# Q transposed on VectorE in 32 x 32 squares and carried through DRAM: one edit to a two-stage attention kernel

## The chip, the cores and the metric

The kernel runs on one core of one Trainium2 chip. The metric is the device time of one execution in microseconds (us); the number for a kernel is the median of several runs. Profiles come from one more execution, recorded by the hardware profiler; its span runs from the first to the last instruction.

## The reference, cut to what matters

The input is 4 sequences of 512 tokens with 128 features. First comes a pre-norm causal attention layer with 16 heads of 64 (stage 1). Then come six layers (stage 2), each a windowed attention followed by a feed-forward block:

```
for i in range(6):
    x = attn_layer(shift_tokens(x), Wqkv[i], q_scale[i], k_scale[i], Wo[i]) + x
    x = ffn_layer(shift_tokens(x), ln_g[i], ...) + x

attn_layer:  q, k, v = split(x @ Wqkv)          # 128 -> 3 x (16 heads x 64)
             q = l2norm(q) * q_scale ; k = l2norm(k) * k_scale   # per head
             q, k = rotary with a per-position scale
             window w of 32 queries sees the keys of windows w-1 and w,
             (keys at most 32 back, none ahead), softmax, times v
             out @ Wo
```

All of it is f32. The edit is in stage 2's attention: how Q is brought into the layout that the scores need, how V is laid out by windows, and on which engine the inverse of the l2 norm is begun.

## The kernel before

Stage 1 takes the first 550 us and is not touched. Stage 2 works in units: a unit is 128 tokens of one sequence in one layer, so there are 6 x 4 x 4 = 96. The order of all instructions is written out by hand: `slot(n, ...)` (L900) issues one slot, and in it four units at different ages: the scores, softmax and values of unit n (`u`), the output projection of n - 1 (`prev`), the last steps of Q and K of n + 1 (`nxt`), and the projections and rotary of n + 2 (`new`). Pieces of the feed-forward block are put into slots by the dictionaries `norm`, `move` and `geglu` (L996 on). Each engine carries out its instructions strictly in the order in which they are issued, so an instruction that waits holds back all that is behind it on its engine. There are four units to a sequence, so slots come in fours.

The way of one unit:

- `project` (L535): six f32 products of 128 x 512 on TensorE for Q, K and V (two instructions each, L538), tokens on the partitions of the result.
- `square` (L550) on ScalarE and `sum_squares` (L555) on VectorE: the sums for the norms.
- `rotate` (L558; L560 and L566) on VectorE and `add_rotated` (L577) on GpSimd: the rotary.
- `inverse_norms` (L579): VectorE clamps the 32 sums of each token (L581) and computes the bit-trick seed of the inverse square root (L83, L84 in `rsqrt`), then GpSimd does three Newton steps of four small operations (L86 to L89). `over_norm` (L584, L585) multiplies on GpSimd, first Q, then K.
- `transpose_q` (L661) and `transpose_k` (L666): eight 128 x 128 transposes on TensorE each (L656), copied out of PSUM by ScalarE (L659). `qT` has the head's features on the partitions and one buffer. The first 32 key columns of `kT` are carried over from the unit before (`carry_k`, L672).
- `scores` (L677): the band mask is put into PSUM by eight bf16 products (L683, the first TensorE instructions of a slot), then 128 small products (L694) add the scores: for each pair of heads `c`, window `j` and head of the pair `h`, 32 queries by 64 keys. VectorE takes the maximum (L704) and subtracts it (L706), ScalarE the exponents (L712).
- `v_windows` (L627): ScalarE copies V out of PSUM into `vt` (L638), tokens on the partitions, with a column of ones beside each head; sixteen DMAs on SyncE's queue (SP) then copy blocks of 32 tokens from SBUF to SBUF into `vw`, so that each window has the keys of the window before and its own on neighbouring partitions. The last window's keys go into the next unit's `vw` as well. `vw` has three buffers, and the first unit of a sequence has its own, `vw_first`, whose missing window is zero.
- `times_v` (L719): 128 small products (L726), VectorE divides by the column of ones (L735, L736), `transpose_o` (L743) and `project_out_2` (L748, L751) follow, `residual` (L753; L759) on VectorE.

In the order of a slot: scores of u, projection 0 of new, exponents of u, the norms of the unit that the slot before left over, feed-forward norm steps, output projection of prev, rotary 0 of new, transposed probabilities of u between the halves of projection 1 of new, `times_v` of u, rotary 1 of new, `transpose_q` of nxt, projection 2 of new, `transpose_k` of nxt, `v_windows` of new, `carry_k`, feed-forward pieces, `transpose_o` of u.

Tiles of one tag share buffers in turn: `t1` has four, taken by the two squares and the two rotary products of a unit.

Of the kernel before, what the change touches and what calls it, by code (L numbers as in the profile page):

```python
# [23 lines left out]
W = 32  # L24
# [8 lines left out]
def body(ctx: ExitStack, tc: tile.TileContext, a, out: bass.AP):  # L33
# [15 lines left out]
    small = ctx.enter_context(tc.tile_pool(name="small", bufs=4))  # L49
    def tmpt(n=S):  # L50
        return tmp.tile([P, n], F32, tag="tmp", name="tmp_t")
# [128 lines left out]
    with tc.manual_schedule():  # L180
# [218 lines left out]
        def residual1(b, y):  # L399
            nc.vector.tensor_tensor(x1T[b], y, x0T[b], ALU.add)  # L400
# [88 lines left out]
    s2a = ps2a = s2b = s2 = ps_one = kT_first = vw_first = vts = None  # L489
# [89 lines left out]
    def inverse_norms(u):  # L579

        nc.vector.tensor_scalar(u.ss, u.ss, 1e-24, None, ALU.max)  # L581
        rsqrt(u.ss, 2 * HEADS, nc.gpsimd)
# [16 lines left out]
    def second_step():  # L599

        nonlocal s2b, ps_one, kT_first, vw_first, vts
        steps[1].close()
        s2b = ctx.enter_context(tc.tile_pool(name="s2b", bufs=1))
        ps_one = ctx.enter_context(tc.tile_pool(name="ps2b", bufs=1, space=PSUM))


        vts = [s2b.tile([P, 2, NC, HD + 1], F32, tag=f"vt{j}", name=f"vt{j}") for j in range(2)]
        for t_ in vts:
            nc.gpsimd.memset(t_[:, :, :, HD : HD + 1], 1.0)
        vw_first = s2b.tile([P, NW, NC, HD + 1], F32, tag="vw_first", name="vw_first")  # L610
        for c in range(2):
            nc.gpsimd.memset(vw_first[c * HD : c * HD + W, 0], 0.0)
        kT_first = s2b.tile([P, NC, W + P], F32, tag="kT_first", name="kT_first")
        nc.gpsimd.memset(kT_first[:, :, 0:W], 0.0)
# [12 lines left out]
    def new_vw(u):  # L627
        if u.T == 0:
            return vw_first
        return s2b.tile([P, NW, NC, HD + 1], F32, tag="vw", name="vw", bufs=3)  # L630

    def v_windows(u, nxt):


        vt = vts[u.n % 2]
        src = u.p[2].rearrange("p (c a d) -> p a c d", a=2, d=HD)
        for c in range(2):
            nc.scalar.copy(vt[:, c, :, 0:HD], src[:, c])  # L638
        if u.T == 0:
            u.vw = new_vw(u)  # L640
        if nxt is not None:
            nxt.vw = new_vw(nxt)
        for j in range(NW):
            rows = slice(j * W, (j + 1) * W)
            for c in range(2):
                nc.sync.dma_start(out=u.vw[c * HD + W : (c + 1) * HD, j], in_=vt[rows, c])
                if j + 1 < NW:
                    nc.sync.dma_start(out=u.vw[c * HD : c * HD + W, j + 1], in_=vt[rows, c])
                elif nxt is not None:
                    nc.sync.dma_start(out=nxt.vw[c * HD : c * HD + W, 0], in_=vt[rows, c])  # L650
# [10 lines left out]
    def transpose_q(u):  # L661
        u.qT = s2b.tile([P, NC, P], F32, tag="qT", name="qT", bufs=1)
        for g in range(2):
            transposed(u.r[0], g, u.qT, 0)
# [12 lines left out]
    def scores(u):  # L677
# [13 lines left out]
        for c in range(NC):  # L691
            for j in range(NW):
                for h in range(2):
                    mm(  # L694
                        sc[j * W : (j + 1) * W, h, c * 2 * W : (c + 1) * 2 * W],
                        lhsT=u.qT[h * HD : (h + 1) * HD, c, j * W : (j + 1) * W],
# [174 lines left out]
    def first_slot():  # L871
# [26 lines left out]
        v_windows(new, units[1])  # L898

    def slot(n, norm, move, geglu):  # L900
# [47 lines left out]
        if n == -1:  # L948
            residual1(B - 1, y)
        if u:  # L950
            times_v(u, 0)
            times_v(u, 1)
# [7 lines left out]
        if nxt:  # L960
            transpose_q(nxt)
        if new:
            do_project(new, 2, 0, 2 if geglu else 1)
        if new and geglu:
            v_windows(new, follower(new))
        if nxt:
            transpose_k(nxt)
        if new and not geglu:
            do_project(new, 2, 1)
            v_windows(new, follower(new))  # L970
# [116 lines left out]
def _constants(n):  # L1087
# [41 lines left out]
    return {"tabs": tabs, "band": band, "pen": pen, "ident16": ident16}  # L1129
# [49 lines left out]
```

## Time and profile before

| what | us |
|---|---|
| median of 3 runs (2192.52 to 2196.64) | 2193.21 |
| span of the profiled execution | 2189.6 |
| TensorE (PE) busy in it | 2137.6 |
| VectorE (DVE) | 1721.8 |
| GpSimd (POOL) | 1509.3 |
| ScalarE (ACT) | 1381.4 |

The runs' time is 3.6 us above the span; no run's time was taken of the profiled execution itself, so this is how the two stand to each other. Mean granted TensorE clock: 0.994 of full speed. DMA moved 125.77 MB, 57 GB/s over the span.

How to read it: a group of instructions is named by its line, engine, operation and tiles (`out<-in`), with how many there were, their busy time and the mean of one; behind the bar stands the idle time of the engine just before them and what ended it. PE are the products, PEld the loads of their stationary operand, which run beside products. The chain is followed back from the last instruction: at each step to what released it, or to the instruction before it on its engine. In an answer in order of time, a row has start, length, engine, line and operation; in brackets stands the idle time before it with its releaser. In a table by stretches, a row has the stretch and its length, then busy us and number of instructions for PE, PEld, DVE, ACT and POOL, the granted TensorE clock, the busy share of the DMA engines, and GB/s.

### The profile page before, as it was taken

What the parts mean: (1) busy time and instruction counts of PE and PEld (TensorE: products, weight loads), DVE (VectorE), ACT (ScalarE), POOL (GpSimd) and SP (SyncE); (2) the same over time, 40 slices, a digit from 0 to 9 for tenths busy, and PEclk for the clock granted to TensorE, in tenths of its full rate; (3) what the DMA queues carried; (4) which work ended last, traced back from release to release, by engine and by line L of the source; (5) the groups of instructions that cost most, each with busy time, mean ns of one, the idle gap of its engine ahead of it and who ended that gap; (6) DMA issues with size and microseconds to landing.
All of it is one profiled execution on the core that took longest, in us unless ns stands there. A gap on an engine that the chain in (4) does not pass through costs nothing.

```text
span 2189.6 us, 82509 instructions
## 1 busy us (share of the span) xinstructions
PE 2137.6 (98%) x35150; PEld 1432.0 (65%) x35150; DVE 1721.8 (79%) x2501; ACT 1381.4 (63%) x2677; POOL 1509.3 (69%) x2281
## 2 busy tenths in 40 slices
PE   7999999999999999999999999999999999999998
PEld 5665555555666666766666666766666666666665
DVE  4766766667778888888888888888888888888884
ACT  4665656665455667766667666676666676666763
POOL 2554545555787787787787777877787777778772
PEclk8999999999999999999999999999999999999999
DMA  3000000000322232232332223323232233323220
GB/s 121 1 1 1 1 1 1 1 1 1 77 64 66 66 93 73 70 74 61 92 78 64 72 68 93 75 62 78 67 100 65 65 76 83 86 65 74 62 71 26
DMA packets 91064, 125.77 MB, mean 57 GB/s; under 512 B 25422, under 2 KB 39500, under 8 KB 90700
## 3 DMA queue, kind: packets, MB, share of 16 engines
q1 hardware_dynamic: 89996, 118.79, 21.8%
q8 instruction: 280, 4.59, 0.9%
q10 hardware_dynamic: 704, 1.70, 0.2%
q14 instruction: 84, 0.69, 0.1%
HBM read 20.31 MB, written 1.05 MB: 10 GB/s over the span
## 4 chain that ended last, share of the span: by engine, by line
PE 89%; DVE 7%; POOL 2%; issue 1%; ACT 1%; DMA 0%; SPq 0%; POOLq 0%; DVEq 0%; ACTq 0%
PE ps_proj L538 21%; PE ps_one L656 15%; PE ps_one L751 7%; PE ps_att L726 6%; PE ps_att L694 6%; PE ps_sc L298 6%; PE ps_o L383 5%; PE ps_pt L363 5%; PE ps_proj L815 3%; PE ps_proj L795 3%; PE ps_proj L796 3%; PE ps_att L683 1%; PE ps_pj L277 1%; PE ps_pj L267 1%; PE ps_pj L261 1%
## 5 line engine op out<-in xcount | busy, mean ns | idle before, releaser
L577 POOL TENSOR_TENSOR rot<-rot,t 128x1024 f32<-128x1024 f32 x192 | 454.2, 2366 | 179.6 <-DVE t L566 161.9
L538 PE MATMUL ps_proj<-wqkv,xs 128*128 128x512 f32 x1152 | 569.3, 602 | 1.8 <-issue 1.3
L352 POOL TENSOR_TENSOR pr<-pr,den 128x1024 f32<-128x1024 f32 x128 | 240.9, 1893 | 247.5 <-DVE den L349 237.7
L585 POOL TENSOR_TENSOR rot<-rot,ss 128x1024 f32<-128x1024 f32 x192 | 361.8, 1905 | 7.4
L550 ACT ACTIVATE sq<-ps_proj 128x1024 f32<-128x1024 f32 x192 | 196.5, 1024 | 177.1 <-PE ps_proj L538 152.7
L538 PEld LDWEIGHTS ps_proj<-wqkv,xs 128*128 128x128 f32 x1152 | 188.2, 190 | 104.8 <-issue 95.0
L560 DVE TENSOR_TENSOR rot<-ps_proj,lt 128x1024 f32<-128x1024 f32 x192 | 233.7, 1217 | 6.8 <-ACT sq L550 6.5
L566 DVE TENSOR_TENSOR t<-ps_proj,lt 128x1024 f32<-128x1024 f32 x192 | 233.1, 1214 | 0.0
L555 DVE TENSOR_REDUCE ss<-sq 128x16 f32<-128x1024 f32 x192 | 232.2, 1210 | 0.0
L338 ACT ACTIVATE pr<-ps_sc,nm 128x128 f32<-128x128 f32 (+3 forms) x448 | 220.3, 509 | 11.8 <-DVE nm L325 8.6
L656 PEld LDWEIGHTS ps_one<-ident,rot 128*128 128x128 f32 x1536 | 173.0, 141 | 71.1 <-issue 46.8
L656 PE MATMUL ps_one<-ident,rot 128*128 128x128 f32 x1536 | 207.5, 278 | 9.2 <-POOL rot L585 4.9
L325 DVE TENSOR_REDUCE nm<-ps_sc 128x2 f32<-128x1024 f32 x128 | 155.9, 1218 | 62.9 <-PE ps_sc L313 62.9
L751 PEld LDWEIGHTS ps_one<-aT,wo 128*128 128x128 f32 x1536 | 182.9, 192 | 23.7 <-issue 21.1
L659 ACT COPY pT<-ps_one 128x512 f32<-128x512 f32 x192 | 110.1, 586 | 136.8 <-PE ps_one L656 136.8
L751 PE MATMUL ps_one<-aT,wo 128*128 128x128 f32 x1536 | 189.1, 276 | 0.4 <-DVE rs L113 0.3
L735 DVE RECIPROCAL rden<-ps_att 128x8 f32<-128x8 f32 x192 | 39.0, 203 | 182.1 <-PE ps_att L726 181.9
L659 ACT COPY qT<-ps_one 128x512 f32<-128x512 f32 x192 | 103.5, 589 | 108.9 <-PE ps_one L656 108.8
L638 ACT COPY vt<-ps_proj 128x512 f32<-128x512 f32 x192 | 103.2, 590 | 98.3 <-PE ps_proj L538 91.9
L86 POOL TENSOR_TENSOR yt<-y 128x32 f32<-128x32 f32 (+2 forms) x384 | 87.7, 228 | 112.1 <-DVE y L84 66.2
L363 PEld LDWEIGHTS ps_pt<-ident,pr 128*128 128x128 f32 x1024 | 117.3, 141 | 58.5 <-issue 47.7
L704 DVE TENSOR_REDUCE mx<-ps_att 128x16 f32<-128x1024 f32 x96 | 117.0, 1219 | 35.8 <-PE ps_att L694 35.5
(174 smaller groups left out, 4194.5 us busy)
## 6 DMA issues: line engine op xcount, KB each, us to landing
vw<-vt SPq DMA_DIRECT2D x1152, 65.0 KB
vw_first<-vt SPq DMA_DIRECT2D x336, 65.0 KB
wqkv<-in_wqkv_dram SPq DMA_DIRECT2D x18, 512.0 KB
wo<-in_wo_dram SPq DMA_DIRECT2D x6, 512.0 KB
w<-in_w_dram SPq DMA_DIRECT2D x6, 341.0 KB
xr<-in_x_dram SPq DMA_DIRECT2D x3, 256.0 KB
scales<-in_scales_dram SPq DMA_DIRECT2D x6, 128.0 KB
w<-in_w_dram SPq DMA_DIRECT2D x12, 64.0 KB
```

The costliest lines, as they stand in the source:

```text
L338: nc.scalar.activation(self.pr[:, h, cols], self.sc[:, h, cols], AF.Exp, bias=self.nm[:, part_, h : h + 1], accum_out=self.den[:, part_, h ...
L352: nc.gpsimd.tensor_tensor(self.pr, self.pr, self.den[:, 0].unsqueeze(2).to_broadcast([P, 2, S]), ALU.mult)
L363: nc.tensor.transpose(pt[:, k * P : (k + 1) * P], self.pr[:, h, k * P : (k + 1) * P], ident)
L538: mm(p[:, c, :], lhsT=u.xs[:, u.T * P : (u.T + 1) * P], rhs=wpart[j][:, c * 512 : (c + 1) * 512], start=True, stop=True,)
L555: nc.vector.tensor_reduce(u.ss[:, j * HEADS : (j + 1) * HEADS], heads(u.sq[j]), AX.X, ALU.add)
L560: nc.vector.tensor_tensor(heads(t0), heads(pf), lt[:, u.T, 2 * j].unsqueeze(1).to_broadcast([P, HEADS, HD]), ALU.mult)
L566: nc.vector.tensor_tensor(t1.rearrange("p (h t d) -> p h t d", t=2, d=half), pf.rearrange("p (h t d) -> p h t d", t=2, d=half)[:, :, ::-1, :],
L577: nc.gpsimd.tensor_tensor(u.r[j], u.r[j], u.t1, ALU.add)
L585: nc.gpsimd.tensor_tensor(heads(u.r[j]), heads(u.r[j]), u.ss[:, j * HEADS : (j + 1) * HEADS].unsqueeze(2).to_broadcast([P, HEADS, HD]), AL ...
L656: nc.tensor.transpose(tp[:, c * P : (c + 1) * P], src[:, (4 * g + c) * P : (4 * g + c + 1) * P], ident)
L659: nc.scalar.copy(dst[:, 4 * g : 4 * g + 4, col0 : col0 + P], tp.rearrange("p (c t) -> p c t", c=4))
L751: mm(y[:, 0:P], lhsT=wo_w[0][:, c, :], rhs=u.aT[:, c, :], start=(c == 0), stop=(c == NC - 1))
```

## The change

Three things change in stage 2.

**Q.** VectorE transposes the normalised Q in 32 x 32 squares (one instruction of 128 x 1024), into a tile `blocks` of the tag `t1`. Since a square stays on its 32 partitions, the squares still stand in the wrong places: one DMA writes all 512 KB to a DRAM tile `qd` (two buffers), and four DMAs of 128 KB read it back, each onto 32 partitions of `qT`. `qT` is now ordered by window, then pair of heads. The eight TensorE transposes and two ScalarE copies are gone. The call of `transpose_q` moves up in the slot, from behind rotary 1 of new to ahead of `times_v` of u.

**V.** `vt` is written to a DRAM tile by one DMA (rows are tokens, with 32 rows of zeros ahead of the first), and four DMAs read it into `vw`: even and odd windows, for each head of the pairs. Two DRAM tiles take turns by sequence. Every unit's `vw` now comes from the same two buffers, and nothing is put into the next unit's.

**Inverse norms.** The clamp and the seed are done by GpSimd, in one operation each, ahead of the Newton steps.

```diff
     def inverse_norms(u):
-        nc.vector.tensor_scalar(u.ss, u.ss, 1e-24, None, ALU.max)
-        rsqrt(u.ss, 2 * HEADS, nc.gpsimd)
+        v, n, eng = u.ss, 2 * HEADS, nc.gpsimd
+        eng.tensor_scalar(v, v, 1e-24, None, ALU.max)
+        y = small.tile([P, n], F32, tag=f"y{n}", name="y")
+        t = small.tile([P, n], F32, tag=f"yt{n}", name="yt")
+        eng.tensor_scalar(y.bitcast(I32), v.bitcast(I32), -0.5, 1597463007.0, ALU.mult, ALU.add)
+        for k in range(3):
+            eng.tensor_tensor(t, y, y, ALU.mult)
...
     def second_step():
...
-        vw_first = s2b.tile([P, NW, NC, HD + 1], F32, tag="vw_first", name="vw_first")
-        for c in range(2):
-            nc.gpsimd.memset(vw_first[c * HD : c * HD + W, 0], 0.0)
+        vds = [dram.tile([W + S, 2, NC * (HD + 1)], F32, tag=f"vd{j}", name=f"vd{j}") for j in range(2)]
+        for d_ in vds:
+            nc.sync.dma_start(out=d_[0:W], in_=a["zeros"])
...
-    def v_windows(u, nxt):
+    def v_windows(u):
-        vt = vts[u.n % 2]
+        vt, vd = vts[u.n % 2], vds[u.n // NT % 2]
...
-        for j in range(NW):
-            rows = slice(j * W, (j + 1) * W)
+        r0 = u.T * P
+        nc.sync.dma_start(out=vd[r0 + W : r0 + W + P], in_=vt.rearrange("p a c d -> p a (c d)"))
+        u.vw = s2b.tile([P, NW, NC, HD + 1], F32, tag="vw", name="vw", bufs=2)
+        for odd in range(2):
+            rows = vd[r0 + odd * W : r0 + odd * W + P].rearrange("(j k) a x -> a k j x", k=2 * W)
             for c in range(2):
-                nc.sync.dma_start(out=u.vw[c * HD + W : (c + 1) * HD, j], in_=vt[rows, c])
-                if j + 1 < NW:
-                    nc.sync.dma_start(out=u.vw[c * HD : c * HD + W, j + 1], in_=vt[rows, c])
-                elif nxt is not None:
-                    nc.sync.dma_start(out=nxt.vw[c * HD : c * HD + W, 0], in_=vt[rows, c])
+                nc.sync.dma_start(
+                    out=u.vw[c * HD : (c + 1) * HD, odd::2].rearrange("p j c d -> p j (c d)"), in_=rows[c]
+                )
...
     def transpose_q(u):
-        u.qT = s2b.tile([P, NC, P], F32, tag="qT", name="qT", bufs=1)
-        for g in range(2):
-            transposed(u.r[0], g, u.qT, 0)
+        blocks = s2a.tile([P, 4, NC, W], F32, tag="t1", name="blocks", bufs=4)
+        nc.vector.transpose(
+            out=blocks.rearrange("p b c d -> p (b c d)"),
+            in_=u.r[0].rearrange("p (c b d) -> p b c d", b=4, d=W),
+        )
+        qd = dram.tile([NW, W, 4, NC * W], F32, tag="qd", name="qd", bufs=2)
+        nc.sync.dma_start(out=qd.rearrange("a i b x -> (a i) (b x)"), in_=blocks.rearrange("p b c d -> p (b c d)"))
+        u.qT = s2b.tile([P, NW, NC, W], F32, tag="qT", name="qT", bufs=1)
+        for b_ in range(4):
+            nc.sync.dma_start(
+                out=u.qT[b_ * W : (b_ + 1) * W].rearrange("p a c d -> p a (c d)"),
+                in_=qd[:, :, b_].rearrange("a i x -> i a x"),
+            )
...
     def scores(u):
...
-                        lhsT=u.qT[h * HD : (h + 1) * HD, c, j * W : (j + 1) * W],
+                        lhsT=u.qT[h * HD : (h + 1) * HD, j, c],
...
     def slot(n, norm, move, geglu):
...
+        if nxt:
+            transpose_q(nxt)
         if u:
             times_v(u, 0)
             times_v(u, 1)
...
-        if nxt:
-            transpose_q(nxt)
         if new:
             do_project(new, 2, 0, 2 if geglu else 1)
```

More of the change, by code (lines that the diff above doesn't have):

```diff
@@ L49, in body @@
     small = ctx.enter_context(tc.tile_pool(name="small", bufs=4))
+    dram = ctx.enter_context(tc.tile_pool(name="dram", bufs=1, space=bass.MemoryType.DRAM))
     def tmpt(n=S):
@@ L488, in body @@
     ps = ctx.enter_context(tc.tile_pool(name="ps2", bufs=1, space=PSUM))
-    s2a = ps2a = s2b = s2 = ps_one = kT_first = vw_first = vts = None
+    s2a = ps2a = s2b = s2 = ps_one = kT_first = vts = vds = None
     def load_part(i, j):
@@ L579, in inverse_norms @@
     def inverse_norms(u):
-        nc.vector.tensor_scalar(u.ss, u.ss, 1e-24, None, ALU.max)
-        rsqrt(u.ss, 2 * HEADS, nc.gpsimd)
+        v, n, eng = u.ss, 2 * HEADS, nc.gpsimd
[5 more added lines that the diff above has]
+            eng.tensor_tensor(t, y, y, ALU.mult)
+            eng.tensor_tensor(t, t, v, ALU.mult)
+            eng.tensor_scalar(t, t, -0.5, 1.5, ALU.mult, ALU.add)
+            eng.tensor_tensor(y if k < 2 else v, y, t, ALU.mult)
     def over_norm(u, j):
@@ L599, in second_step @@
     def second_step():
-        nonlocal s2b, ps_one, kT_first, vw_first, vts
+        nonlocal s2b, ps_one, kT_first, vts, vds
         steps[1].close()
@@ L625, in new_kT @@
         return s2.tile([P, NC, W + P], F32, tag="kT", name="kT", bufs=2)
[L627 to L630, printed above, removed]
-    def v_windows(u, nxt):
-        vt = vts[u.n % 2]
+    def v_windows(u):
+        vt, vd = vts[u.n % 2], vds[u.n // NT % 2]
         src = u.p[2].rearrange("p (c a d) -> p a c d", a=2, d=HD)
@@ L638, in v_windows @@
             nc.scalar.copy(vt[:, c, :, 0:HD], src[:, c])
[L639 to L642, printed above, removed]
-        for j in range(NW):
-            rows = slice(j * W, (j + 1) * W)
-            for c in range(2):
-                nc.sync.dma_start(out=u.vw[c * HD + W : (c + 1) * HD, j], in_=vt[rows, c])
-                if j + 1 < NW:
-                    nc.sync.dma_start(out=u.vw[c * HD : c * HD + W, j + 1], in_=vt[rows, c])
-                elif nxt is not None:
-                    nc.sync.dma_start(out=nxt.vw[c * HD : c * HD + W, 0], in_=vt[rows, c])
+        r0 = u.T * P
[3 more added lines that the diff above has]
+            rows = vd[r0 + odd * W : r0 + odd * W + P].rearrange("(j k) a x -> a k j x", k=2 * W)
+            for c in range(2):
+                nc.sync.dma_start(
+                    out=u.vw[c * HD : (c + 1) * HD, odd::2].rearrange("p j c d -> p j (c d)"), in_=rows[c]
+                )
     def transposed(src, g, dst, col0):
@@ L897, in first_slot @@
         do_project(new, 2)
-        v_windows(new, units[1])
+        v_windows(new)
     def slot(n, norm, move, geglu):
@@ L964, in slot @@
         if new and geglu:
-            v_windows(new, follower(new))
+            v_windows(new)
         if nxt:
@@ L969, in slot @@
             do_project(new, 2, 1)
-            v_windows(new, follower(new))
+            v_windows(new)
         if n == -1:
@@ L1128, in _constants @@
     ident16 = np.eye(P).astype(ml_dtypes.bfloat16)
-    return {"tabs": tabs, "band": band, "pen": pen, "ident16": ident16}
+    zeros = np.zeros((W, 2, NC * (HD + 1)), f)
+    return {"tabs": tabs, "band": band, "pen": pen, "ident16": ident16, "zeros": zeros}
 def kernel(**inputs):
```

## The prediction

> **What bounds the kernel now.** I read the page first, then the chain of work that ended last, then the groups, then the order in time of one slot, and last the places where TensorE stood still.
>
> ```profile
> span 2189.6 us, 82509 instructions
> PE 2137.6 (98%) x35150; PEld 1432.0 (65%) x35150; DVE 1721.8 (79%) x2501; ACT 1381.4 (63%) x2677; POOL 1509.3 (69%) x2281
> PE 89%; DVE 7%; POOL 2%; issue 1%; ACT 1%; DMA 0%; SPq 0%; POOLq 0%; DVEq 0%; ACTq 0%
> ```
>
> PE is busy for 98% of the span and is 89% of the chain; DMA is nothing in it. So an instruction that leaves PE shortens the kernel, as long as no wait takes its place. The layers are 96 slots, one per unit of 128 tokens; a slot begins with the band matmuls of L683. From the first (559.71) to the last (2149.78) it is 1590 us, 16.74 us for each of 95 slots. They come in fours of 15.87, 16.85, 17.49 and 16.26 us (medians).
>
> The order in time of the slot that starts at 1226.24, by engine (start, length, line):
>
> ```profile
> 1226.24 0.41 PE L683 MATMUL ps_att<-band,ident 64*32 64x512 bf16 x8
> 1226.47 1.69 PE L694 MATMUL ps_att<-kT_first,qT 64*32 64x64 f32 x128
> 1234.39 1.59 PE L726 MATMUL ps_att<-vw_first,pT 64*32 64x65 f32 x128
> 1235.91 1.09 PE L656 MATMUL ps_one<-ident,rot 128*128 128x128 f32 x8
> 1236.84 1.88 PE L538 MATMUL ps_proj<-wqkv,xs 128*128 128x512 f32 x4
> 1242.11 0.41 PE L683 MATMUL ps_att<-band,ident 64*32 64x512 bf16 x8
> ...
> 1230.04 1.23 DVE L706 TENSOR_TENSOR pr<-ps_att,mx 128x1024 f32<-128x1024 f32 x1
> 1231.23 1.23 DVE L560 TENSOR_TENSOR rot<-ps_proj,lt 128x1024 f32<-128x1024 f32 x1
> 1232.37 0.28 DVE L759 TENSOR_TENSOR xT<-ps_one,xT 128x128 f32<-128x128 f32 x1
> 1232.57 1.22 DVE L566 TENSOR_TENSOR t<-ps_proj,lt 128x1024 f32<-128x1024 f32 x1
> 1235.41 0.21 DVE L735 RECIPROCAL rden<-ps_att 128x8 f32<-128x8 f32 x1 [1.62 <-PE ps_att L726]
> ...
> 1232.16 3.76 POOL L585 TENSOR_TENSOR rot<-rot,ss 128x1024 f32<-128x1024 f32 x2
> ```
>
> Two things are to be seen. The eight Q transposes hold PE from 1235.91 to 1236.84. And Q is wanted early: it is normalised by the first half of L585 (to 1234.0), and the next scores read it at 1242.3.
>
> **Part 1: off PE and ACT.** The Q transposes go: 0.93 us a slot, 95 x 0.93 = 88 us, all of it on the chain. (By the chain's share, 15% on L656's 3072 transposes, it is 0.107 x 8 = 0.86 us.) PE alone would need 16.74 - 0.93 = 15.81 us. ACT loses two qT copies (0.59 us each); it has gaps in every slot, so I count nothing.
>
> **Part 2: clamp and seed to GpSimd.** DVE loses L581 (1.36 us mean), L83 (0.26) and L84 (0.20), 1.8 us a slot. GpSimd gains two small operations, at 0.22 us (L88) and a gap of 0.1 each about 0.6 us, and no longer waits for DVE's seed. GpSimd is busy some 13 of 16.7 us. PE waits for neither; I count nothing by itself. It lets DVE begin L704 as soon as the scores end; that enters below.
>
> **Part 3: V through DRAM.** 15.5 DMAs of 65 KB a unit become one write of 520 KB and four reads of 130 KB. V is made two slots before L726 reads it: with about 9 us for write and reads (below) against over 25 us, it is hidden. SP issues ten DMAs a slot instead of 15.5. Queued order on SP matters: Q's write and reads stand ahead of V's, and V's of the slot before are done (write 4 us after its copy, four issues of 0.6 us) some 4 us into the next slot, before Q's write is wanted. Cost nothing; without that cover V would cost as much as Q does.
>
> **Part 4: Q's new way, which is the forecast.** DVE's transpose waits for L585, SP's write waits for the transpose, the four reads wait for the write, and the scores, at the head of PE's queue, wait for the reads; all PE work of the slot is queued behind them. Counted from a slot's first PE instruction:
>
> - DVE ends L566 at 7.5, 8.3, 7.9 and 7.55 us in the four kinds of slot. In the first two DVE came late to L704 (2.54 and 2.78 against 2.0, behind L581); without that the mean is 7.5. Q's L585 ends at 7.8, 8.1, 7.35 and 6.6, and since GpSimd does not wait for PE here, each us by which PE is late takes one off: it ends first once PE waits. So 7.5.
> - The transpose, 128x1024 f32, is not in the trace. Nearest: L555, one input of that size, 1.21 us. Below: L125, SBUF to SBUF, 0.57 for half the size, so 1.1. Above: GpSimd's 2.37, or a wait as of L581, which takes 0.17 us with GpSimd idle and up to 2.26 beside it. I take 1.2: 8.7 us. It stands ahead of L735, where DVE idles anyway (1.62 us above).
> - The write of 512 KB to DRAM. Nearest: the last output, 256 KB in two DMAs, first issued at 2186.43; the bytes move from 2187.25 to 2188.4 and the span ends at 2189.6, 3.2 us after the issue. Another 256 KB at its 290 GB/s is 0.9: 4.1. Below: the 0.85 us to the first byte, 1.8 us of bytes and the 0.5 us between last byte and reader that the scales load shows: 3.15.
> - Four reads of 128 KB. An issue takes 0.6 (L646), so the fourth starts 1.8 us after the first. From issue to reader: 3.3 us for the 128 KB of scales (two rows below, behind a V transfer), 2.8 for the first load of x (0.75 to 3.55). I take 1.8 + 3.0 = 4.8; bounds 1.35 + 2.8 = 4.15 (issues of 0.45 as at the start) and 5.3.
>
> ```profile
> 1839.45 0.54 SPq L170 DMA_DIRECT2D scales<-in_scales_dram  x1
> 1842.73 2.37 POOL L172 TENSOR_TENSOR lt<-tabs,scales 128x1024 f32<-128x1024 f32 x1 [1.36 <-DMA scales<-in_scales_dram]
> 2186.43 0.90 SPq L836 DMA_DIRECT2D out_dram<-rot  x2
> ```
>
> Sum: 8.7 + 0.1 + 4.1 + 4.8 = 17.7 us from one slot's scores to the next. That is more than PE's 15.8 and more than today's 16.74. The loop closes through DVE (scores, L704, L706, L560, L566, transpose), so a late start is not made up. PE would stand still for 17.7 - 15.8 = 1.9 us at each slot's head.
>
> **What such a stop does to PE's clock.** The trace has 26 stops over 0.7 us. After the 1.90 us before 2145.36, the 2.84 before 8.60 and the 2.91 before 673.99 the granted clock is 0.5 for 3 to 13 us; after those up to 1.61 us it stays 1.00.
>
> ```profile
> 671.10:674.00 2.90, 0.01 (x4) 0.01 (x4) 2.90 (x4) 1.20 (x3) 1.99 (x11) 0.97 0.32 75
> 674.00:677.00 3.00, 3.00 (x137) 2.51 (x137) 1.59 (x2) 0.00 (x0) 2.37 (x1) 0.50 0.38 89
> 677.50:680.00 2.50, 2.50 (x16) 1.74 (x15) 2.40 (x7) 1.15 (x2) 0.37 (x2) 1.00 0.45 107
> ```
>
> (The seventh number is PE's clock.) The slot at 673.99 shows the price: L566 ends 8.54 us in, against 7.55 in its kind, and the slot takes 17.59 against 16.26. So a slowed slot adds 1.0 us to the loop. Stops of 1.9 us lie at the edge; I take every second slot slowed: 18.2 us. The excess is 18.2 - 16.74 = 1.46, times 95 = 139 us. The profiled execution: 2189.6 + 139 = 2328.6; the median lies 3.6 above that span, so 2332 us.
>
> Two pages of the Trainium skill differ from these rows. "DMA: Bandwidth & Descriptors", Anatomy of one DMA, gives 2.0 us plus bytes at 436 GB/s for a DMA (of GpSimd's path): by that, an estimate, write 3.2 and last read 2.3 us; with the issues the loop is 16.1 us and the kernel some 60 us faster. "TensorE: Matmul & The Clock Gate", Part 1, lets the clock fall after an idle window of about 3.4 us: by that no stop here would slow PE, and the loop stays at 17.7; the trace has it at 0.5 after 1.9 us.
>
> **Rivals.**
> - *The transfers are quick enough (faster).* The point is the way from transpose to scores: 8.0 us gives today's slot (8.7 + 8.0), 7.1 hides it all. At the lower bounds of the rows, 0.1 + 3.15 + 4.15 = 7.4, the slot is 16.1: 95 x -0.64 = -61, 2132 us; all hidden, 2105. For it: the DMA engines are busy for 30% of the layers. Against: the two roundtrips in a row that the output and the scales show.
> - *A stop without the slow clock.* 17.7: 95 x 0.96 = +91, 2284 us. For it: stops up to 1.61 us left the clock alone, and the wait splits unevenly among slots.
> - *A longer way.* Write 4.3, reads 5.3, transpose held behind the second L585, every slot slowed: 8.7 + 1.0 + 9.7 = 19.4, and with a held transpose up to 20.6. 19.4 gives +253, 2446 us.
> - *GpSimd becomes the bound*: 13.6 us of work in a slot of 15.8 or more; I give it no share of its own.
> - *It does not do what it says*: the built order shows the eight matmuls gone, one transpose on DVE and five DMAs for Q in each slot, so no.
>
> **How the numbers follow.** Stop with the clock slowed in part (2290 to 2390): 0.46. Stop without (2200 to 2290): 0.20. Longer (above 2390): 0.16. Faster: 0.15. Equal within 0.2% (what a measurement of this kernel can tell from no change; it needs 8.0 within 0.05): 0.03. Range 2135 to 2445: from the rows' lower bounds to the longer way at 19.4. Slower by over 0.2% 0.82, same 0.03, faster 0.15.
>
> **What would show it.** Right: L694 (L705 after) waits for the qT transfer at nearly every slot's head, DMA appears in the chain, PE's share falls to about 88%, slots of about 18 us, the granted clock 0.5 in part of the slots. Transpose: about 1.2 us, ahead of the reciprocals. Write: some 4 us from issue to the first read's issue; reads 4.8 us from there to L694. Wrong: no idle time before the scores and slots below 16.7 us; or a clock of 1.00 throughout; or a wait on V or on GpSimd ahead of the one on Q.

## The result, and the profile after

The changed kernel takes 2279.73 us (median of 4 runs, 2274.09 to 2282.22) against 2192.86 us for the kernel before on the same chip: a ratio of 1.038, 95% interval 1.036 to 1.040. The forecast was 2332 us. The profiled execution's span grows from 2189.6 to 2277.5 us, by 87.9 us. Line numbers from here on are those of the changed kernel, some 10 above those of before (scores L694 and L705, maximum L715, values L737, reciprocals L746, `over_norm` L594, Q's transpose L664, its write L669 and reads L672).

The page of the changed kernel: span, busy time, DMA, the chain's shares by engine, the transpose's group, and the transfers with their time from issue to landing.

```profile
span 2277.5 us, 79327 instructions
...
PE 2092.4 (92%) x34382; PEld 1364.7 (60%) x34382; DVE 1683.3 (74%) x2309; ACT 1275.1 (56%) x2485; POOL 1555.8 (68%) x2471
...
DMA packets 157928, 280.79 MB, mean 123 GB/s; under 512 B 17006, under 2 KB 80236, under 8 KB 157548
...
PE 60%; DMA 11%; POOL 11%; DVE 10%; issue 4%; SPq 3%; ACT 1%; POOLq 0%; DVEq 0%; ACTq 0%
...
L664 DVE STREAM_TRANSPOSE blocks<-rot 128x1024 f32<-128x1024 f32 x96 | 119.0, 1240 | 29.3 <-POOL rot L594 29.2
...
qd<-blocks SPq DMA_DIRECT2D x96, 512.0 KB, 2.8
qT<-qd SPq DMA_DIRECT2D x384, 128.0 KB, 2.9
```

PE lost its 768 transposes, 88 us by the prediction's count, yet its busy time fell by only 45.2 us: the rest ran slower, at a mean granted clock of 0.979 instead of 0.994. Its idle time rose from 52 to 185 us, by 133. So 133 - 45 = 88. The chain, 89% PE before, now runs through DMA, GpSimd and VectorE for a third of its length.

Where PE stands idle, from the view of waits (us in total, times, longest):

```profile
PE ps_att L705 <- DMA qT<-qd: 77.1, 90, 6.3
...
PE ps_proj L539 <- DVE rden L746: 47.9, 76, 1.8
```

The first is the wait that was forecast: the scores wait for Q. The second was not: projection 2 of new waits for VectorE's reciprocals, which free the PSUM bank that it writes. Before, the eight Q transposes stood between `times_v` and projection 2 and covered that time. Both are seen in one slot, in order of time:

```profile
1216.48 1.51 PE L737 MATMUL ps_att<-vw,pT 64*32 64x65 f32 x128
...
1217.22 1.25 DVE L664 STREAM_TRANSPOSE blocks<-rot 128x1024 f32<-128x1024 f32 x1 [1.40 <-POOL rot L594]
...
1218.39 0.17 DVE L746 RECIPROCAL rden<-ps_att 128x8 f32<-128x8 f32 x1
...
1218.49 0.34 SPq L669 DMA_DIRECT2D qd<-blocks  x1
...
1219.43 1.95 PE L539 MATMUL ps_proj<-wqkv,xs 128*128 128x512 f32 x4 [1.44 <-DVE rden L746]
...
1221.39 1.76 SPq L672 DMA_DIRECT2D qT<-qd  x4
...
1224.78 0.41 PE L694 MATMUL ps_att<-band,ident 64*32 64x512 bf16 x8
...
1225.83 1.46 PE L705 MATMUL ps_att<-kT,qT 64*32 64x64 f32 x126 [0.55 <-DMA qT<-qd]
```

VectorE's transpose waits 1.40 us for GpSimd's normalization, and the reciprocals are queued behind it. From its end (1218.47) the write is issued at once, the first read 2.9 us later, the four reads some 0.44 us apart, and the scores go on at 1225.83: 7.4 us for the whole way.

By stretch of the layers, in the same two executions: the first eight slots took 131.9 us before and 159.8 after (+27.9), the other 87 took 1458.2 and 1509.8 (+51.6), the end behind the last scores 39.8 and 47.9 (+8.1). The mean slot is 17.57 us (16.74 before). Sixteen slots are longer than 18.6 us (one before); below they are called long. The others grew little: from the ninth slot on the medians of the four kinds are 16.50, 17.38, 17.78 and 16.10 us, in the mean 16.94 (before 16.62); this is called the ordinary slot.

### The profile page after: what moved, and what is told of

Same layout as the page of the kernel before. It is cut to its first block, busy times and chain, and to the rows that moved or that the text cites. A ratio compares the mean times of both kernels' runs of the same rounds, so it can differ in the third digit from the quotient of the medians.

```text
span 2277.5 us, 79327 instructions
## 1 busy us (share of the span) xinstructions
PE 2092.4 (92%) x34382; PEld 1364.7 (60%) x34382; DVE 1683.3 (74%) x2309; ACT 1275.1 (56%) x2485; POOL 1555.8 (68%) x2471
## 4 chain that ended last, share of the span: by engine, by line
PE 60%; DMA 11%; POOL 11%; DVE 10%; issue 4%; SPq 3%; ACT 1%; POOLq 0%; DVEq 0%; ACTq 0%
PE ps_proj L539 15%; DMA qT<-qd 7%; PE ps_sc L299 5%; PE ps_o L384 5%; PE ps_one L657 5%; PE ps_one L762 5%; PE ps_att L705 5%; PE ps_pt L364 5%; DMA qd<-blocks 4%; POOL rot L578 3%; SPq L672 3%; POOL rot L594 3%; PE ps_att L737 2%; PE ps_proj L826 2%; DVE on L747 2%
## 5 line engine op out<-in xcount | busy, mean ns | idle before, releaser
L539 PE MATMUL ps_proj<-wqkv,xs 128*128 128x512 f32 x1152 | 593.4, 624 | 52.8 <-DVE rden L746 47.9
L578 POOL TENSOR_TENSOR rot<-rot,t 128x1024 f32<-128x1024 f32 x192 | 453.3, 2361 | 240.9 <-DVE t L567 156.9
L594 POOL TENSOR_TENSOR rot<-rot,ss 128x1024 f32<-128x1024 f32 x192 | 361.7, 1905 | 7.4
L539 PEld LDWEIGHTS ps_proj<-wqkv,xs 128*128 128x128 f32 x1152 | 193.6, 195 | 174.7 <-issue 122.6
L561 DVE TENSOR_TENSOR rot<-ps_proj,lt 128x1024 f32<-128x1024 f32 x192 | 233.8, 1218 | 23.4 <-ACT sq L551 21.2
L567 DVE TENSOR_TENSOR t<-ps_proj,lt 128x1024 f32<-128x1024 f32 x192 | 233.4, 1215 | 18.8 <-POOL rot L578 18.8
L715 DVE TENSOR_REDUCE mx<-ps_att 128x16 f32<-128x1024 f32 x96 | 117.6, 1225 | 172.5 <-PE ps_att L705 172.3
L737 PEld LDWEIGHTS ps_att<-vw,pT 64*32 64x32 f32 x12288 | 131.4, 105 | 83.8 <-ACT pT L660 71.3
L705 PE MATMUL ps_att<-kT,qT 64*32 64x64 f32 x9216 | 126.0, 233 | 60.1 <-DMA qT<-qd 55.5
L737 PE MATMUL ps_att<-vw,pT 64*32 64x65 f32 x12288 | 150.4, 225 | 8.6 <-issue 8.0
L705 PEld LDWEIGHTS ps_att<-kT,qT 64*32 64x32 f32 x9216 | 111.2, 108 | 78.3 <-DMA qT<-qd 52.3
L664 DVE STREAM_TRANSPOSE blocks<-rot 128x1024 f32<-128x1024 f32 x96 | 119.0, 1240 | 29.3 <-POOL rot L594 29.2
```

Source lines behind the costliest of these rows:

```text
L539: mm(p[:, c, :], lhsT=u.xs[:, u.T * P : (u.T + 1) * P], rhs=wpart[j][:, c * 512 : (c + 1) * 512], start=True, stop=True,)
L561: nc.vector.tensor_tensor(heads(t0), heads(pf), lt[:, u.T, 2 * j].unsqueeze(1).to_broadcast([P, HEADS, HD]), ALU.mult)
L567: nc.vector.tensor_tensor(t1.rearrange("p (h t d) -> p h t d", t=2, d=half), pf.rearrange("p (h t d) -> p h t d", t=2, d=half)[:, :, ::-1, :],
L578: nc.gpsimd.tensor_tensor(u.r[j], u.r[j], u.t1, ALU.add)
L594: nc.gpsimd.tensor_tensor(heads(u.r[j]), heads(u.r[j]), u.ss[:, j * HEADS : (j + 1) * HEADS].unsqueeze(2).to_broadcast([P, HEADS, HD]), AL ...
L705: mm(sc[j * W : (j + 1) * W, h, c * 2 * W : (c + 1) * 2 * W], lhsT=u.qT[h * HD : (h + 1) * HD, j, c], rhs=u.kT[h * HD : (h + 1) * HD, c, j ...
```

## The experiments

The theory on record: Q's way to the scores is the bound (letter C in later expectations). Its rivals: the doubled traffic slows everything (B); V or the norms take a share; and, after the first four runs, that the reciprocals queued behind VectorE's transpose hold TensorE (A), and that VectorE's part of the slot is next (D). "Slot" is the mean of 95 in the profiled execution, "long" the number of slots over 18.6 us, "clock" the mean granted TensorE clock of that execution. Ratios are to the kernel before, run on the same chip.

| run | median us | ratio, 95% interval | slot | long | clock |
|---|---|---|---|---|---|
| change | 2279.73 | 1.038 (1.036 to 1.040) | 17.57 | 16 | 0.979 |
| 1 norms alone | 2181.24 | 0.994 (0.993 to 0.996) | 16.62 | 0 | 0.996 |
| 2 V alone | 2178.25 | 0.993 (0.991 to 0.994) | 16.57 | 1 | 0.995 |
| 3 Q alone | 2338.54 | 1.066 (1.064 to 1.069) | 18.16 | 32 | 0.972 |
| 4 stale Q | 2277.64 | 1.038 (1.036 to 1.040) | 17.64 | 23 | 0.975 |
| 5 stale Q, old place | 2243.19 | 1.023 (1.021 to 1.024) | 17.24 | 12 | 0.978 |
| 6 K first | 2296.98 | 1.049 (1.046 to 1.052) | 17.71 | 23 | 0.968 |
| 7 early norms | 2230.02 | 1.017 (1.015 to 1.019) | 17.11 | 7 | 0.990 |
| 8 early norms, K first | 2265.23 | 1.033 (1.030 to 1.035) | 17.41 | 17 | 0.979 |
| 9 early norms, place of the change | 2288.57 | 1.040 (1.037 to 1.043) | 17.71 | 24 | 0.973 |
| 10 norms and V | 2174.24 | 0.989 (0.987 to 0.990) | 16.53 | 1 | 0.996 |
| 11 fill in the first layer | 2281.95 | 1.039 (1.037 to 1.041) | 17.56 | 14 | 0.986 |
| 12 reads on two queues | 2274.12 | 1.035 (1.032 to 1.037) | 17.59 | 18 | 0.982 |

**Runs 1 to 3: each part alone, put into the kernel before.** Run 1 takes `inverse_norms` of the change, run 2 `second_step` and `v_windows`, run 3 `transpose_q`, its new place and the new index of `qT`:

```diff
# run 1
-        nc.vector.tensor_scalar(u.ss, u.ss, 1e-24, None, ALU.max)
-        rsqrt(u.ss, 2 * HEADS, nc.gpsimd)
+        eng.tensor_scalar(v, v, 1e-24, None, ALU.max)   # eng = nc.gpsimd
...
# run 2
-            v_windows(new, follower(new))
+            v_windows(new)
...
# run 3
+        if nxt:
+            transpose_q(nxt)
         if u:
             times_v(u, 0)
```

> The kernel before with only the clamp and the seed of the inverse norms on GpSimd. Late-Q theory (Q's way through DRAM makes TensorE wait ahead of the scores): this part costs and gives nothing of itself, since TensorE waits for neither, so 2185 to 2197 us, with VectorE some 175 us less busy. Lost-cover theory (a second wait stands ahead of projection 2): the same. Rival, GpSimd's two operations of 0.3 us per unit delay the norms and with them the Q and K transposes: slower by 0.3 to 0.6 us a slot, 2220 to 2250 us.

> The kernel before with only V's key blocks through DRAM. Late-Q theory: V is made two slots early, so its two trips are hidden: 2185 to 2200 us. Traffic theory (the doubled DMA traffic and the DRAM trips hold up other loads, instruction fetch among them): V brings half of the new traffic, so it should show a good part of the 87 us: 2215 us or more, with more idle time of TensorE that has no releaser.

> The kernel before with only Q through VectorE and DRAM, at its new place in the slot. Late-Q theory: nearly the whole loss is here; VectorE keeps the clamp (1.36 us a slot beside GpSimd), which makes its transpose later, so as slow as the change or slower: 2275 to 2330 us. Traffic theory: with half of the new traffic, clearly faster than the change: 2210 to 2245 us.

Norms alone and V alone are each faster than before, by 0.6 and 0.7%, both a little below the ranges expected; Q alone is slower by 6.6%, a little above its range and more than the whole change. So all of the loss is Q's, and the two other parts give some back: beside Q's new way more (1.066 to 1.038) than without it (run 10), which no run divides up. V's part moves 180.17 MB in place of 125.77, a third of what the change adds and not the half that was expected, and is faster: this traffic by itself slows nothing, and no wait on V stands in PE's list. Of the norms' gain, 6.6 us lie in the first eight slots (131.9 to 125.3 in the profiles), where VectorE reaches the scores sooner; of V's gain 14.4 us lie in the 87 others, in small pieces whose cause these runs do not settle.

**Run 4: the scores use the Q of the unit before (the scores, and so the output, are not the reference's).** Nothing in the scores can then wait for a Q that is on its way.

```diff
-        u.qT = s2b.tile([P, NW, NC, W], F32, tag="qT", name="qT", bufs=1)
+        u.qT = s2b.tile([P, NW, NC, W], F32, tag="qT", name="qT", bufs=2)
...
-                        lhsT=u.qT[h * HD : (h + 1) * HD, j, c],
+                        lhsT=units[max(u.n - 1, 0)].qT[h * HD : (h + 1) * HD, j, c],
```

> The changed kernel with two buffers for the transposed Q, and the scores of a unit take the Q of the unit before it (so the scores are of the wrong queries; all instructions and DMAs remain, only the wait for this slot's Q is gone). Late-Q theory alone: the wait ahead of the scores was the loss, so the kernel shows the 0.93 us a slot that left TensorE: about 2105 us. Late Q and lost cover: the wait of some 0.5 to 1.4 us for VectorE's reciprocals ahead of projection 2 stays, so 2145 to 2180 us. Traffic theory: still above 2190 us.

The time did not move, and for a while that looked as if late Q were no cause. But PE's waits had only moved: the one for the reciprocals rose from 47.9 to 120.1 us. And part of that is the run's own: in 18 slots the transpose starts only when GpSimd has ended L578, for which it never waits in the changed kernel. With `qT` in two buffers the transpose may get a buffer of the tag `t1` that L578 still reads; no run shows whether that is the reason. One of these slots in order of time:

```profile
1229.24 2.35 POOL L578 TENSOR_TENSOR rot<-rot,t 128x1024 f32<-128x1024 f32 x1
1231.62 1.25 DVE L664 STREAM_TRANSPOSE blocks<-rot 128x1024 f32<-128x1024 f32 x1 [5.42 <-POOL rot L578]
...
1233.83 3.46 PE L539 MATMUL ps_proj<-wqkv,xs 128*128 128x512 f32 x4 [3.70 <-DVE rden L746]
```

The four products of projection 2 then take 3.46 us instead of 1.95: the slow clock. The 18 slots take 372 us, 66 us more than 18 of the mean of the others (17.03, without those right behind). Run 4 shows how dearly the reciprocals pay for a transpose that waits ahead of them; it can't say what late Q costs.

**Run 5: as run 4, with VectorE's transpose back at its old place, behind the reciprocals, the rotation and the sums.** (The scores again use the Q of the unit before.)

```diff
-        if nxt:
-            transpose_q(nxt)
         if u:
             times_v(u, 0)
...
             sum_squares(new, 1)
+        if nxt:
+            transpose_q(nxt)
```

> The changed kernel with the scores of a unit using the Q of the unit before it (so the result is not the reference's), qT in two buffers, and VectorE's transpose back at the place where the Q transposes stood, behind both reciprocals, the rotation and the sums of squares. The DMA traffic and every instruction are as in the changed kernel; only what waits behind what differs. Theory A (VectorE's transpose stands ahead of the reciprocals and waits in its queue for GpSimd's norms, the reciprocals hold the PSUM bank of projection 2, and the stop of TensorE halves its clock): that wait falls to the 0.5 us that the reciprocals need by themselves, 95 x 0.5 = 48 us of the 88 us that the removed transposes free, so 2193 - 88 - 12 (norms, measured) + 48 = 2140 us, range 2105 to 2185. Theory B (the doubled traffic stretches code fetches and everything that TensorE reads, or the clock sinks for another reason): the time stays at 2240 us or more, as with the transpose ahead of the reciprocals (2278).

By its number 2243 us would do for theory B; the slots say otherwise. From the ninth on, the medians of the four kinds are 15.38, 16.35, 16.99 and 15.78 us (before: 15.87, 16.85, 17.49, 16.26): without the wait for Q, and with 39.9 us in 87 stops left of the one for the reciprocals (0.42 us a slot), a slot is half a microsecond shorter than before, in spite of all the traffic. But ten slots take 22.7 to 25.5 us, 245.5 in total, 85 more than ten of 16.1. Rows of two of them, in order of time:

```profile
781.20 0.59 SPq L171 DMA_DIRECT2D scales<-in_scales_dram  x1
...
786.34 2.35 POOL L173 TENSOR_TENSOR lt<-tabs,scales 128x1024 f32<-128x1024 f32 x1 [6.71 <-DMA scales<-in_scales_dram]
...
792.49 2.08 PE L103 MATMUL ps_one<-tmp_t,avg 128*128 128x512 f32 x2 [6.02 <-POOL tmp_t L161]
...
970.02 0.59 SPq L505 DMA_DIRECT2D w<-in_w_dram  x1
...
975.46 2.04 PE L806 MATMUL ps_proj<-hT,w 128*128 128x512 f32 x2 [5.06 <-DMA w<-in_w_dram]
```

SP issues in order. Q's reads wait there for Q's write, V's reads for V's write, and whatever is queued behind comes late: in five slots the scales of the next layer (GpSimd waits 6.6 us in the mean, PE 6.0 behind it), in five the weights of the feed-forward block (PE waits 3.8 to 6.5 us). Take the 85 us away and 2158 is left, near theory A's 2140. Traffic that slows every slot is refuted.

**Run 6: K's transposes ahead of projection 2**, as a new cover for the reciprocals.

```diff
+        if nxt:
+            transpose_k(nxt)
         if new:
             do_project(new, 2, 0, 2 if geglu else 1)
...
-        if nxt:
-            transpose_k(nxt)
```

> The changed kernel with TensorE's transposes of K moved ahead of projection 2 (1.04 us of work), where before the removed transposes of Q stood. Theory A (the missing cover of the reciprocals is what stops TensorE): the stop ahead of projection 2 goes in most slots, TensorE keeps its clock there, and the late Q alone is left: about 2200 us, range 2170 to 2245. Theory C (Q's way to the scores is the bound, as predicted): the freed time is given back at the scores, 2265 to 2290 us.

The wait for the reciprocals is gone from PE's list, and the time rose to 2297 us, a little past what theory C expected. The wait at the scores grew from 77.1 to this:

```profile
PE ps_att L705 <- DMA qT<-qd: 98.3, 116, 6.5
```

Theory A falls for the changed kernel as it stands: what is saved at projection 2 is given back at the scores. The ordinary slots stay as they were (the medians of the four kinds 16.90 us in the mean, 16.94 in the changed kernel), the long ones go from 16 to 23 and the clock sinks to 0.968. Q's way sets the pace. (Stops ahead of L705 without a releaser grew too, from 6.2 to 26.7 us; their cause is open.)

**Run 7: the norms early.** Both sums of squares and GpSimd's norms for Q go ahead of K's rotation; the transpose goes to the slot's beginning.

```diff
             exponents(u)
+        if nxt:
+            transpose_q(nxt)
...
-        if nxt:
-            transpose_q(nxt)
...
             sum_squares(new, 0)
+            sum_squares(new, 1)
+            inverse_norms(new)
+            over_norm(new, 0)
             rotate(new, 1)
             add_rotated(new, 1)
-            sum_squares(new, 1)
...
-            norms = [lambda: inverse_norms(new), lambda: over_norm(new, 0), lambda: over_norm(new, 1)]
+            norms = [lambda: over_norm(new, 1)]
```

> The changed kernel with the chain of Q pulled forward: both sums of squares ahead of K's rotation on VectorE, the inverse norms and Q's normalization ahead of K's rotation on GpSimd, so that Q is normalized at the end of the slot before, and VectorE's transpose right behind the subtraction of the scores' maximum, some 5 us earlier and ahead of nothing that waits for it. Theory A and the late Q together: neither the reciprocals nor the scores wait any more, only the missing cover of 0.5 us ahead of projection 2 is left: 2140 us, range 2105 to 2180. Theory B (traffic): 2240 us or more. If GpSimd is the next bound (its rotation of K comes later, and FFN work stands behind it): 2190 to 2230 us with TensorE waiting for K's transposes.

2230 us: the best with Q's new way and true scores, more than half of the loss gone, with the same traffic. The number is at the upper end of the third case, though PE does not wait for K's transposes. The scores' wait for Q falls to 6.8 us; PE now waits for VectorE: for the reciprocals (32.8), for the rotation ahead of the band's products (22.6), for L105 (21.2) and for L124 (16.8). VectorE's transpose stands in the loop from the scores to the next scores, and it still waits for GpSimd's L594, so by the chain the two engines bound this kernel in turn. The chain's shares and the transpose's wait, then two pieces of one slot in order of time:

```profile
PE 53%; DVE 20%; POOL 19%; issue 6%; DMA 1%; ACT 1%; SPq 0%; POOLq 0%; DVEq 0%; ACTq 0%
...
DVE blocks L664 <- POOL rot L594: 36.5, 37, 7.5
```

```profile
1174.72 1.25 DVE L664 STREAM_TRANSPOSE blocks<-rot 128x1024 f32<-128x1024 f32 x1 [0.24 <-POOL rot L594]
1175.89 0.65 DVE L124 TENSOR_TENSOR hT<-tmp_t,ps_one 128x512 f32<-128x512 f32 x1
...
1176.46 1.21 DVE L561 TENSOR_TENSOR rot<-ps_proj,lt 128x1024 f32<-128x1024 f32 x1
1176.68 0.63 PE L657 MATMUL ps_one<-ident,pr 128*128 128x128 f32 x4 [0.74 <-DVE hT L124]
```

**Run 8: runs 6 and 7 together** (both diffs above).

> Early norms and the transposes of K ahead of projection 2 together. Theory A and the late Q: the cover is back as well, so the slot falls to what TensorE has to do without Q's transposes: 2193 - 88 = 2105 us, with about half of it held back by VectorE and GpSimd 2125 us, range 2100 to 2165. Theory B (traffic): 2230 us or more. If GpSimd is the next bound: 2180 to 2220 us, TensorE waiting for K.

2265 us, slower than run 7; only theory B's "or more" takes it in, and that theory can't tell why run 7 takes 2230 with the same bytes. PE reaches the next scores sooner and waits there for VectorE's rotation to free the bank (`L694 <- DVE t L567` 22.6 us in run 7, 46.2 here). PE's stops in the layers become fewer and longer (194 of them, 122.9 us in total, in run 7; 137 and 138.2 us here; 11 and 28 of them over 1.6 us), the long slots go from 7 to 17 and the clock from 0.990 to 0.979. Here a cover that does not shorten the loop was worth nothing, and the fewer, longer stops cost more. (Of their time 31.3 us, ahead of L705, have no releaser in the profile, against 13.9 in run 7.)

**Run 9: early norms, the transpose at the place of the change.** (Run 7 without its first two hunks.)

> Early norms as in the run before (both sums of squares, the inverse norms and Q's normalization ahead of K's rotation), but VectorE's transpose left at the place that the change gave it, ahead of the reciprocals. There VectorE idled 1.3 to 1.9 us in the run with early norms, and Q is now normalized 3 to 5 us before, so the transpose waits for nothing and holds nothing. Theory D (what is left with early norms is VectorE's part of the loop scores, maximum, exponents, P, times V, reciprocals, rotation, scores, which the transpose behind the subtraction lengthened by 1.25 us): the slot falls from 17.1 us to about 16.2 us, 2230 - 95 x 0.9 = 2145 us, range 2115 to 2170. Theory C (Q's way to the scores is the bound): the transpose ends as late as VectorE's rotation lets it, Q lands about when the scores want it or up to 1 us later, and the time stays at 2190 to 2240 us. Theory B (traffic): 2230 us or more.

2289 us, no better than the change: theory D's number fails, and theory C's mechanism holds at a higher price than expected. Nothing holds the transpose now (4.2 us in total), but it comes later than in run 7, and Q is late again. The waits, and below them PE around a stop, then the stretches around it (the seventh number is PE's clock):

```profile
PE ps_att L705 <- DMA qT<-qd: 80.2, 85, 6.4
```

```profile
1374.16 0.39 PE L705 MATMUL ps_att<-kT,qT 64*32 64x64 f32 x2 [2.40 <-DMA qT<-qd]
1375.25 2.03 PE L705 MATMUL ps_att<-kT,qT 64*32 64x64 f32 x126 [0.70 <-DMA qT<-qd]
1377.20 3.78 PE L539 MATMUL ps_proj<-wqkv,xs 128*128 128x512 f32 x4
```

```profile
1363.00:1371.30 8.30, 7.57 (x154) 4.43 (x152) 7.35 (x9) 5.42 (x8) 6.98 (x11) 1.00 0.56 185
1371.30:1377.00 5.70, 2.60 (x138) 2.07 (x136) 0.75 (x1) 3.18 (x6) 5.12 (x9) 0.74 0.87 226
1377.00:1382.00 5.00, 5.00 (x34) 2.76 (x18) 2.61 (x3) 0.98 (x2) 2.98 (x3) 0.61 0.37 118
1382.00:1388.00 6.00, 5.57 (x138) 4.12 (x137) 4.66 (x6) 3.19 (x5) 2.37 (x1) 1.00 0.80 194
```

A stop of 2.40 us is followed by a clock of 0.61; the same four products take 3.78 us instead of 1.95, and this slot takes 23.4 us against 17.9, the median of its kind.

**Run 10: norms and V without Q**, the candidate for the fastest version (the diffs of runs 1 and 2).

> The kernel before with two of the three parts: the inverse norms on GpSimd and V's key blocks through DRAM; Q stays with TensorE's transposes. Each part alone was 0.6 to 0.7% faster. If the two gains are independent: 2193 - 12 - 16 = 2165 us, range 2155 to 2175. If both take away the same few stops: 2172 to 2182 us. The theory that V's traffic costs TensorE something once other waits are gone: 2180 us or more.

```profile
span 2169.2 us, 80396 instructions
...
PE 2122.4 (98%) x35150; PEld 1425.6 (66%) x35150; DVE 1568.4 (72%) x2213; ACT 1378.3 (64%) x2677; POOL 1556.2 (72%) x2471
```

2174 us, 1.1% faster than before and the fastest of all. By ratio the gains nearly add up (0.6 and 0.7%); the time lies in both expected ranges, 2155 to 2175 and 2172 to 2182, so it does not tell them apart.

**Run 11: TensorE filled while it waits, in the first layer.** The band's products are issued nine times over for units 1 to 7; the repeats write the same values.

```diff
-        for j in range(NW):
+        for j in list(range(NW)) * (9 if u.n in range(1, 8) else 1):
             for h in range(2):
```

> The changed kernel with the band's small matmuls ahead of the scores of units 1 to 7 issued nine times over instead of once (the repeats write the same values): 8 x 0.41 = 3.3 us of useless work for TensorE in each of these slots, at the place where it stands waiting for Q. There the changed kernel had slots of 19.4 to 24.3 us with the clock at 0.5 to 0.76 in part of each, against 15.3 to 16.8 us before. If the stop's clock and not the late Q itself makes these slots long: with the stop filled they fall to about 18 us, the granted clock of that stretch goes from 0.87 to above 0.95, and the time to 2262 to 2272 us. If the clock has no part in it: the slots stay at 19 to 21 us or grow by the work that is added, 2278 to 2295 us.

The stretch of these slots, first in the changed kernel, then in run 11:

```profile
540.00:700.00 160.00, 128.48 (x2275) 81.87 (x2272) 104.02 (x119) 55.64 (x85) 106.87 (x181) 0.87 0.46 133
```

```profile
540.00:700.00 160.00, 136.97 (x2883) 88.47 (x2880) 109.23 (x126) 59.75 (x90) 116.18 (x204) 0.96 0.50 144
```

The clock there rose from 0.87 to 0.96 and the first eight slots fell from 159.8 to 150.5 us, although PE did 23 us of useless work in them. So, in the one execution profiled of each, part of the length of these slots was the slow clock behind the stops. The median did not move, though (2281.95 us; the other 87 slots, whose program is the same, took 8.3 us more in that execution), so the expected 2262 to 2272 is missed: the run shows that the clock has a part in it, but no gain in time.

**Run 12: run 9 with two of the four reads issued by ScalarE's queue.**

```diff
-            nc.sync.dma_start(
+            (nc.sync, nc.scalar)[b_ % 2].dma_start(
                 out=u.qT[b_ * W : (b_ + 1) * W].rearrange("p a c d -> p a (c d)"),
```

> Early norms with the transpose at the change's place (the run at 2289), and two of Q's four reads issued by ScalarE's queue instead of all four by SyncE's, so that the last one goes out 2 x 0.43 = 0.9 us sooner; ScalarE stands idle at that point, 2.3 to 2.8 us ahead of its copy of V. In the run at 2289 the waits of the scores for Q were 0.2 to 1.2 us in most slots, over 2 us where a slowed slot came before. Theory C (Q's way to the scores is the bound of that kernel, and a stop costs more than its length because TensorE's clock is halved behind it): most of the waits go, and the slowed slots with them: 16.4 to 17.2 us a slot instead of 17.7, that is 2165 to 2240 us, central 2205. If the loop through VectorE is the bound and the wait only its shadow, as with the transpose behind the subtraction: 2225 to 2250 us at best. If the reads are limited by what they move and not by their issue: 2275 us or more.

2274 us, 0.5% below run 9 by ratio, with intervals that just touch; the expected 2165 to 2240 is missed. The issues end 0.9 us sooner, but a read now takes 3.6 us (SyncE's) and 4.0 us (ScalarE's) to land instead of 2.9, so Q gains a few tenths. PE's wait for Q does fall from 80.2 to 31.1 us, and another takes its place:

```profile
PE ps_one L657 <- ACT kT L660: 39.0, 29, 3.4
```

ScalarE now waits in its queue for Q's write, and its copies of V and K stand behind that wait. In the worst slots the write itself is late, and PE stops up to 3.4 us for K's copy.

## Why the prediction was right, and where it was off

- **Sign, mechanism and place: right.** L705 waits for Q 90 times, at the heads of 62 of the 96 slots (forecast: of nearly all); DMA is 11% of the chain; PE's busy share falls to 92% (forecast: about 88). Q alone makes the loss (run 3). Starting Q's way earlier, by early norms and an earlier place of the transpose together, removes more than half of it (run 7); early norms alone do not (run 9).
- **PE's 0.93 us a slot, ScalarE's copies: right.** They are gone, and in run 5 a slot is 0.49 us shorter than before with 0.42 us of waiting for the reciprocals left, 0.91 together.
- **The loop of 17.7 us: right in its first part, 0.7 us too long in its second.** The band's products at a slot's head do not wait for Q, so the loop has to be taken from where the scores go on, 0.9 us behind the first of them in the median. From there, from the ninth slot on, the transpose ends after 8.7 us in the median, as counted, and 9.0 in the mean. Its wait for GpSimd's L594 (29.2 us, 34 times, 0.3 us a slot in the mean) had been ruled out by "it ends first once PE waits". From the transpose's end to the scores it is 8.3 us in the median, where 9.0 was counted (in the 61 slots after which the scores waited for it 7.2 to 10.4, median 8.4). The write lies below its term (4.1 counted, 3.2 median from issue to first read issue, near the lower bound 3.15), the reads nearly at theirs (0.43 us an issue instead of 0.6, 2.9 us to land). 8.7 + 8.3 is 17.0, the ordinary slot of the result, 16.94.
- **So the forecast's error is the loop, and not the clock.** The loop was to add 0.96 us to each of 95 slots, 91 us; the medians of the four kinds grew by 0.32, 31 us. The step "I take every second slot slowed: 18.2 us" put 48 us on top. That is near in size: all slots together stand 59.5 us above the medians of their kinds, 11.1 before, so 48 more. It is wrong in form: not every second slot by 1.0, but 16 of 95 by 1.2 to 7.8 us, 56 in all: the first six of the layers, five at every sixteenth slot (14, 30 and so on), and five others. Nor is all of it clock: time multiplied by what was missing from the full granted clock comes to 36 us in the layers (4 before), 34 of it in the long slots. Small terms make up the rest: 8.1 us behind the last scores were not counted, and the runs' time is 1.8 us above the span, not 3.6.
- **The rival without the slow clock, 2284 us, came nearest (2280 measured) by luck:** it had the ordinary slots too long and no long ones.
- **"Transfers quick: 7.4 us gives 2132" was wrong in its reasoning, not only in its chance.** In the slot shown the way is 7.4 us, and the loop is 17.0 all the same (the scores before had started at 1208.80), because the transpose, held for 1.40 us by GpSimd, ends 9.7 us behind the scores' start. The rival took 8.7 there as fixed.
- **"It stands ahead of L735, where DVE idles anyway": wrong where the transpose has to wait.** It holds the reciprocals, they hold a PSUM bank, and PE stops at projection 2 (47.9 us). The removed transposes were the cover of the reciprocals; what they hid was not asked. Run 6 shows that in the changed kernel this wait is not the bound; in runs 4 and 5, without the wait for Q, it is PE's largest (120.1 us, in part the run's own, and 39.9).
- **"V: cost nothing" and "norms: nothing by itself": too low by a gain.** Alone they are 0.7 and 0.6% faster. No wait on V stands ahead of Q's. One on GpSimd does, at the transpose (29.2 us), which the text named as a sign of being wrong: "GpSimd becomes the bound" had no share, and GpSimd's part of the chain went from 2 to 11%, as one leg of the loop.
- **"After those up to 1.61 us it stays 1.00": no rule.** In the changed kernel the clock is 0.50 for 3.4 us behind two stops of 0.99 and 0.79 us (1347.70 to 1351.10), and 1.00 behind one of 2.22 us (2201.70 to 2205.00). The length of one stop does not settle it.
- **Rules of the skill.** The Trainium skill's "TensorE: Matmul & The Clock Gate", Part 1, has the clock low after an idle window of about 3.4 us; here it is 0.61 behind a stop of 2.40 us (run 9) and 0.50 behind the two short ones, so the measured rows decide. "DMA: Bandwidth & Descriptors", Anatomy of one DMA, with its figures for GpSimd's path, gives an estimate of 3.2 us for the write and 2.3 for a read; 3.2 and 2.9 were measured. By its figures, with the transpose's 8.7 us, the loop was 16.1 us; 17.0 was measured.

**Still open.** Some stops have no releaser in the profile ("issue"), such as 2.62 us ahead of the second product of L539 at 828.23 in the changed kernel; what they wait for was not found. Why the slots at every sixteenth place and the five others are long was not followed up. Why V alone gains is not settled, nor what late Q alone would cost in the changed kernel without run 4's own waits. Whether the early norms with Q on a quicker way would beat the kernel before was not tried further.

## What to carry to other kernels

Before you take work off the engine that bounds the kernel, ask what that work was covering: the instruction behind it may be waiting for something that it hid. When an operation moves to another engine, its position there decides: an instruction that waits at the head of an in-order queue (VectorE's transpose, SyncE's reads, ScalarE's reads in run 12) charges its wait to all that stands behind it. A loop that runs once per slot is judged as a whole, from one scores to the next: making a cover or one leg shorter moves the wait unless the longest loop itself gets shorter.

## What the runs showed of the hardware that was not expected

- A stop costs more than its length: one of 2.40 us and the 5 us behind it had a granted clock of 0.74 and 0.61 in the two stretches that cover them, 10.7 us (run 9). But its length alone does not decide: two stops of 0.99 and 0.79 us were followed by 0.50, one of 2.22 us by 1.00 (changed kernel).
- 43% more DMA bytes (180.17 MB against 125.77) did not slow TensorE (run 2, 0.7% faster).
- VectorE's transpose of 128 x 1024 f32 in squares of 32 takes 1.24 us, hardly more than a plain pass over that size (1.21), which the prediction could only estimate.
- The four reads of 128 KB from one queue land 2.9 us after each issue; from two queues 3.6 and 4.0, so most of the time won at the issue is lost again (run 12).
